# One level of block products in the last projection, its l by a product with ones, and a normalisation in one operation

## The chip, the cores and the metric

The kernel runs on one core of a Trainium2 chip. The metric is the device time of one execution in microseconds (us), the median of several; a profiled execution gives the span from first to last instruction, some 1.8 us less than its time. The mean granted TensorE clock was 0.996 to 1.000 of full speed in every run, and every run of a kernel with more than one was in the fast state. A kernel with a single run has no state of its own, which is said where it matters. The calls ran on different chips, and the median of the kernel before was 3249.5 to 3251.2 us in them; differences are taken within a call, and where kernels of different calls are compared, the text says so. Engines are written PE (matmul), PEld (its weight loads), DVE (VectorE), ACT (ScalarE), POOL (GpSimd) and SP (a DMA queue).

## The reference

```python
# x: (16, 512, 32, 32) float32
mu, var = mean and variance of x over each of 8 groups of 64 channels
xn = (x - mu) * rsqrt(var + 1e-5) * gamma + beta
q, k, v = split(qkv_w @ xn + qkv_b)               # 1x1 convolution, 3 x 512 channels
attn = softmax(q^T k * 128**-0.5)                 # 4 heads of 128, 1024 tokens
out = x + proj_w @ (attn-weighted v) + proj_b     # 1x1 convolution, residual
```

Everything is float32.

## The kernel before

The sixteen images follow each other in one stream: while the score products (`s`) and weighted sums (`po`) of one image run, the projection of the image before and the statistics, normalisation and v, q, k of the next are woven in between. `l` is the denominator of the softmax, a sum of exponentials for each token. Large products are made from block products: two levels for q, k and the projection (49 products of 256 columns in place of 64), one level for v (7 products of half size in place of 8). Block products need sums of blocks of the activations (`t1`, `t2`, ...) and of the results, which DVE makes. `warm` are matmuls without use that PE runs at the start while it waits.

The parts that the change touches:

```python
def apply(self, xn, x, mu, sc, c, on_scalar):          # first image: two passes
    nc.vector.tensor_scalar(xn, x, mu[c], sc[c], ALU.subtract, ALU.mult)
    if on_scalar:
        nc.scalar.activation(xn, xn, AF.Identity, bias=beta)
...
def normalise(b, c, half=None):                        # other images: two passes, both on ACT
    nc.scalar.activation(t, t, AF.Identity, bias=nmu[:, i])
    nc.scalar.activation(t, t, AF.Identity, bias=beta_sb[:, i], scale=sc[:, i])
...
def denominators(b, h):                                # l, every head of every image
    # DVE: transpose, reduce, three small additions, transpose
    nc.vector.reciprocal(r, l[:, 3, :])                # 32x32
    nc.sync.dma_start(row..., r)                       # to DRAM ...
    nc.sync.dma_start(rinv[b, h], row.to_broadcast((P, N)))   # ... and back as 128 equal rows
    nc.vector.scalar_tensor_tensor(worst, l[:, 3, :], 1.0, r, ALU.mult, ALU.max,
                                   accum_out=spans[:, i : i + 1])
...
# after the last score product: the last image's projection in two levels, nothing beside it
o_blocks(last)
run(groups[0])
divide(last, HEADS - 1)
sums_of_b(ob[last], (2,), (1,))
run(staggered(groups[1:]))
```

`spans` collects max(l, 1/l) of every head. If the total is over 1e20, a second, general path does the whole work again.

## Time and profile before

| what | before |
|---|---|
| time, median of 3 | 3251.3 us (3250.0 to 3251.66) |
| profiled span | 3247.3 us, clock 0.997 |
| PE busy | 3202.9 us, 99% |
| start, until the first v product | 17.71 us |
| one image | mostly 199.47 us |
| tail, from the end of the last score product | 49.67 us |

The span has three parts with different limits, so it is read in three parts. To mark the image borders I use the product `pm`, the first small matmul of an image's statistics, of which there is one an image: the second image has it at 143.42 us, the last at 2933.94. The totals of the page are these (busy us, share of the span, number of instructions):

```profile
PE 3202.9 (99%) x10708; PEld 2011.9 (62%) x10708; DVE 2476.6 (76%) x4425; ACT 1290.0 (40%) x2178; POOL 16.8 (1%) x20
```

They tell that PE is the bound almost everywhere, and nothing of where the one per cent that is not PE lies. That is at the two ends, and the prediction below starts from there.

### The profile page before, as it was taken

The numbers are of one execution on the slowest core, as the hardware profiler recorded it, in microseconds if no ns is written. First come the engines' busy times: TensorE is split into PE (matmuls) and PEld (weight loads), VectorE is DVE, ScalarE is ACT, GpSimd is POOL, SyncE is SP. The second block draws the span as 40 slices with busy tenths as digits, with TensorE's granted clock in tenths as the row PEclk, the third lists the DMA queues.
The fourth block names the chain that finished last, engine by engine and source line by source line (L and its number), as shares of the span: only waits on it lengthen the run. The fifth ranks groups of instructions, "written<-read, shape, count | busy, mean of one in ns | idle before, by whom it ended". The sixth has DMA issues, their size and how long they took to land.

```text
span 3247.3 us, 31121 instructions
## 1 busy us (share of the span) xinstructions
PE 3202.9 (99%) x10708; PEld 2011.9 (62%) x10708; DVE 2476.6 (76%) x4425; ACT 1290.0 (40%) x2178; POOL 16.8 (1%) x20
## 2 busy tenths in 40 slices
PE   7999999999999999999999999999999999999997
PEld 6566666666666666666666666666666666666654
DVE  8858688586886868868687785967859689586886
ACT  2433434334343343434434343443433434344332
POOL 0000000000000000000000000000000000000000
PEclk9999999999999999999999999999999999999998
DMA  5323333233232333333333332333323333233232
GB/s 174 128 79 126 111 104 131 77 118 123 95 129 87 117 111 107 119 103 112 107 114 109 102 123 90 120 108 113 123 80 126 105 111 124 84 114 123 80 115 83
DMA packets 114021, 357.39 MB, mean 110 GB/s; under 512 B 15424, under 2 KB 27200, under 8 KB 113856
## 3 DMA queue, kind: packets, MB, share of 16 engines
q1 hardware_dynamic: 112848, 354.27, 32.2%
q8 instruction: 86, 1.41, 0.2%
q10 hardware_dynamic: 1008, 1.06, 0.1%
q14 instruction: 79, 0.65, 0.1%
HBM read 310.00 MB, written 45.29 MB: 109 GB/s over the span
## 4 chain that ended last, share of the span: by engine, by line
PE 90%; ACT 5%; DVE 3%; DMA 1%; issue 1%; POOL 0%; ACTq 0%; SPq 0%; POOLq 0%; DVEq 0%
PE s L603 25%; PE po L648 25%; PE qk_x L466 12%; PE qk_y L466 9%; PE v_x L545 6%; PE v_y L545 5%; PE pp_x L466 5%; PE pp_y L466 3%; ACT x L232 2%; ACT x L231 2%; DVE tot L615 1%; ACT p L608 1%; DVE pp_r L498 1%; POOL rstd L64 0%; DVE pp_r L481 0%
## 5 line engine op out<-in xcount | busy, mean ns | idle before, releaser
L603 PE MATMUL s<-qk,qk 128*128 128x512 f32 x2048 | 1048.4, 593 | 2.2 <-DVE qk L516 1.3
L648 PE MATMUL po<-p,v 128*128 128x512 f32 x2048 | 1045.3, 593 | 0.7 <-ACT p L608 0.7
L608 ACT ACTIVATE p<-s 128x512 f32<-128x512 f32 x1024 | 611.2, 597 | 1053.2 <-PE s L603 1046.4
L615 DVE TENSOR_TENSOR tot<-tot,p 128x1024 f32<-128x1024 f32 x384 | 468.8, 1221 | 315.3 <-ACT p L608 312.1
L648 PEld LDWEIGHTS po<-p,v 128*128 128x128 f32 x2048 | 387.1, 190 | 455.0 <-issue 431.0
L603 PEld LDWEIGHTS s<-qk,qk 128*128 128x128 f32 x2048 | 386.2, 190 | 93.7 <-issue 37.3
L466 PEld LDWEIGHTS qk_x<-qk_t,w 128*128 128x128 f32 x1344 | 250.6, 190 | 199.4 <-issue 140.2
L466 PE MATMUL qk_x<-qk_t,w 128*128 128x256 f32 x1344 | 358.0, 383 | 1.4 <-ACT qk_u L394 1.1
L394 ACT COPY qk_u<-qk_x 128x512 f32<-128x512 f32 (+1 forms) x256 | 136.4, 533 | 240.6 <-PE qk_x L466 239.5
L466 PE MATMUL pp_x<-pp_t,w_proj 128*128 128x256 f32 x672 | 180.3, 385 | 1.1 <-ACT pp_u L394 1.1
L545 PE MATMUL v_y<-w_v,x 128*128 128x256 f32 x720 | 176.5, 381 | 3.8 <-ACT x L232 3.8
L545 PEld LDWEIGHTS v_y<-w_v,x 128*128 128x128 f32 x720 | 135.3, 190 | 66.3 <-issue 40.2
L481 DVE TENSOR_TENSOR qk_r<-qk_y,qk_u 128x512 f32<-128x512 f32 (+1 forms) x256 | 158.4, 619 | 22.8 <-PE qk_y L466 21.4
L466 PEld LDWEIGHTS pp_x<-pp_t,w_proj 128*128 128x128 f32 x672 | 125.1, 191 | 78.1 <-issue 51.7
L545 PEld LDWEIGHTS v_x<-w_v,xt 128*128 128x128 f32 x720 | 136.8, 190 | 57.0 <-issue 43.0
L545 PE MATMUL v_x<-w_v,xt 128*128 128x256 f32 x720 | 170.1, 379 | 0.0
L466 PE MATMUL qk_y<-x,w 128*128 128x256 f32 x512 | 141.8, 379 | 0.0
L516 DVE SCALAR_TENSOR_TENSOR qk<-qk_r,qkb_sb,qk_r 128x512 f32<-128x512 f32 x192 | 135.4, 745 | 1.5 <-ACT qk_r L479 0.4
L394 ACT COPY pp_u<-pp_x 128x512 f32<-128x512 f32 (+1 forms) x128 | 68.2, 533 | 170.0 <-PE pp_x L466 166.9
L565 DVE TENSOR_TENSOR v<-v_y,v_u 128x512 f32<-128x512 f32 x64 | 43.7, 682 | 114.4 <-ACT v_u L394 69.9
L481 DVE TENSOR_TENSOR qk_r<-qk_y,qk_p 128x512 f32<-128x512 f32 (+1 forms) x128 | 79.1, 618 | 57.1 <-PE qk_y L466 57.1
L466 PEld LDWEIGHTS qk_y<-x,w 128*128 128x128 f32 x512 | 97.3, 190 | 39.7 <-issue 21.8
(144 smaller groups left out, 3499.7 us busy)
## 6 DMA issues: line engine op xcount, KB each, us to landing
w<-kept SPq DMA_DIRECT2D x90, 896.0 KB, 4.5
w_v<-kept_v SPq DMA_DIRECT2D x60, 768.0 KB, 4.5
w_proj<-kept_proj SPq DMA_DIRECT2D x48, 896.0 KB, 4.6
rinv<-row SPq DMA_DIRECT2D x64, 512.0 KB, 3.7
y<-in_x SPq DMA_DIRECT2D x128, 256.0 KB, 3.8
out_y<-y SPq DMA_DIRECT2D x128, 256.0 KB, 2.4
x<-in_x SPq DMA_DIRECT2D x62, 512.0 KB, 4.1
w<-kept SPq DMA_DIRECT2D x30, 448.0 KB, 3.3
```

The lines of the kernel that those rows point to most:

```text
L231: nc.scalar.activation(t, t, AF.Identity, bias=nmu[:, i])
L232: nc.scalar.activation(t, t, AF.Identity, bias=beta_sb[:, i], scale=sc[:, i])
L394: nc.scalar.copy(t[n][:, :width], t["x"][:, :width])
L466: nc.tensor.matmul(acc[:, ts(i, Q)], have["w"][:, i, SLOTS[an], :], inner(i, bn), start=(first and i == 0), stop=True, skip_group_check=True,)
L481: nc.vector.tensor_add(dst, view(a), view(c))
L516: nc.vector.scalar_tensor_tensor(st[b, h][:, ts(half, HALF)], a[:, r, :], qkb_sb[:, i : i + 1], c[:, r, :], ALU.add, ALU.add,)
L545: nc.tensor.matmul(acc[:, ts(g, HC)], xb[b][bn][k][:, ts(2 * jj + g, P)], wi[:, k, :], start=(first and g == 0 and k == 0), stop=(k == KC ...
L565: nc.vector.tensor_add(dst, view(a), view(c))
L603: nc.tensor.matmul(sc, ks[b, h][:, ts(j, P)], qs[b, h][:, ts(half, HALF)], start=True, stop=True)
L608: nc.scalar.activation(ps[s][:, ts(half, HALF)], sc, AF.Exp, scale=SCALE)
L615: nc.vector.tensor_add(tot[b, h], tot[b, h], ps[s])
L648: nc.tensor.matmul(po[b, h][:, i], vs[b, h // 2][:, h % 2, j, :], ps[s][:, i], start=(j == 0), stop=(j == NB - 1),)
```

## The change

Its intent: the tail is bound by DVE and by two transfers, not by PE, so spend PE work to save the others there; the normalisation is one pass where it was two; and the first image's x is to land before the weights.

```diff
-        nc.vector.tensor_scalar(
-            xn, x, mu[:, c : c + 1], sc[:, c : c + 1], ALU.subtract, ALU.mult
-        )
+    def shift(self, mu, sc):                     # sh = beta - mu * sc, 128x4
+        nc.vector.tensor_mul(t, mu, sc)
+        nc.vector.tensor_sub(sh, self.beta, t)
...
+            self.nc.scalar.activation(xn, x, AF.Identity, bias=sh[:, i], scale=sc[:, i])
         else:
+            self.nc.vector.tensor_scalar(xn, x, sc[:, i], sh[:, i], ALU.mult, ALU.add)
... load_x
-            eng = (nc.sync, nc.scalar)[c % 2] if b == 0 else nc.sync
-            eng.dma_start(xs[b, c], x[b, ts(c, P), :])
+            for half in range(NH2 if b == 0 else 1):
+                i = ts(half, HALF) if b == 0 else ds(0, N)
+                nc.sync.dma_start(xs[b, c][:, i], x[b, ts(c, P), i])
... the last head's l
+        for half in range(NH2):
+            nc.tensor.matmul(l, ones_sq, t[:, ts(half, HALF)], start=True, stop=True)
+            nc.vector.reciprocal(r[:, i], l)
+            nc.vector.tensor_mul(os_[b, h][:, i], os_[b, h][:, i], r[:, i])
... and its check
+        nc.vector.reciprocal(l, r[:BLK, :])
+        nc.vector.scalar_tensor_tensor(l, l, 1.0, r[:BLK, :], ALU.mult, ALU.max, accum_out=...)
... the last projection: 28 products of 512 columns, residual and bias already in y
+            mm(x_[r], r, 1, True);  copy(r, "p1")
+        recip = last_division(b, HEADS - 1)
+        sums_of_b(bl, (2,), (1,))
+        ...  products 5, 2, 6 with their additions into y
+        last_span(recip)
+        ...  products 7, 4, 3
... start
-    warm(9, "warm")
+    warm(7, "warm")
```

The diff above leaves out three parts of the change: outside the first image too the halves are normalised with all four first halves ahead (before, tile by tile); in the first image DVE and ACT now take the tiles in turn, and only the first of the four weight sums of v is still placed by an order of its own (`issue_after`), where all four were; the last head's sum of exponentials is added in halves.

The last image's x is loaded into `y` early and the bias added there by ACT; outputs leave from `y` on two queues. The weights of the one-level products are stored once and loaded again for the last image.

More of the change, by code (lines that the diff above doesn't have):

```diff
@@ L49, in group @@
         nc.tensor.matmul(pm[:, :k], self.avg, mean, start=True, stop=True)
-        mu = gn.tile([P, k], F32, tag="mu", name="mu")
-        nc.vector.tensor_copy(mu, pm[:, :k])
         d = gn.tile([P, k], F32, tag="d", name="d")
-        nc.vector.tensor_sub(d, mean, mu)
+        nc.vector.tensor_sub(d, mean, pm[:, :k])
         d2 = gn.tile([P, k], F32, tag="d2", name="d2")
@@ L58, in group @@
         nc.vector.tensor_add(v, d2, mv[:, :, 1])
+        mu = gn.tile([P, k], F32, tag="mu", name="mu")
+        nc.vector.tensor_copy(mu, pm[:, :k])
         pv = self.ps.tile([P, HALF], F32, tag=self.tag, name="pv")
@@ L67, in group, with apply @@
         return mu, sc
-    def apply(self, xn, x, mu, sc, c, on_scalar):
-        nc, beta = self.nc, self.beta[:, c : c + 1]
-        nc.vector.tensor_scalar(
-            xn, x, mu[:, c : c + 1], sc[:, c : c + 1], ALU.subtract, ALU.mult
-        )
+    def shift(self, mu, sc):
+        nc = self.nc
+        t = self.gn.tile([P, self.ncc], F32, tag="t", name="t")
+        nc.vector.tensor_mul(t, mu, sc)
+        sh = self.gn.tile([P, self.ncc], F32, tag="sh", name="sh")
+        nc.vector.tensor_sub(sh, self.beta, t)
+        return sh
+    def apply(self, xn, x, sc, sh, c, on_scalar):
+        i = slice(c, c + 1)
         if on_scalar:
-            nc.scalar.activation(xn, xn, AF.Identity, bias=beta)
+            self.nc.scalar.activation(xn, x, AF.Identity, bias=sh[:, i], scale=sc[:, i])
         else:
-            nc.vector.tensor_scalar(xn, xn, beta, None, ALU.add)
+            self.nc.vector.tensor_scalar(xn, x, sc[:, i], sh[:, i], ALU.mult, ALU.add)
 @with_exitstack
@@ L183, in fast_path @@
     ones = one.tile([BLK, 1], F32, name="ones")
+    ones_sq = one.tile([P, P], F32, name="ones_sq")
     xs, xb, vs, qs, ks, os_, ob = {}, {}, {}, {}, {}, {}, {}
@@ L203, in fast_path @@
     nc.vector.memset(neghalf, -0.5)
+    nc.vector.memset(ones_sq, 1.0)
     for t, src in (
@@ L217, in stats_group, with normalise @@
         mu, sc = norm.group(mvs.pop(b))
-        nmu = None
-        if b > 0:
-            nmu = gn.tile([P, NCC], F32, tag="nmu", name=f"nmu_{b}")
-            nc.vector.tensor_scalar_mul(nmu, mu, -1.0)
-        scaled[b] = mu, sc, nmu
-    def normalise(b, c, half=None):
-        t = xs[b, c] if half is None else xs[b, c][:, ts(half, HALF)]
-        mu, sc, nmu = scaled[b]
-        if nmu is None:
-            norm.apply(t, t, mu, sc, c, True)
-        else:
-            i = slice(c, c + 1)
-            nc.scalar.activation(t, t, AF.Identity, bias=nmu[:, i])
-            nc.scalar.activation(t, t, AF.Identity, bias=beta_sb[:, i], scale=sc[:, i])
+        scaled[b] = sc, norm.shift(mu, sc)
+    def normalise(b, c, half):
+        t = xs[b, c][:, ts(half, HALF)]
+        sc, sh = scaled[b]
+        norm.apply(t, t, sc, sh, c, b > 0 or c % 2 == 1)
     def halves(tiles, prefix):
@@ L297, in fast_path @@
     store["v"] = kept.tile([P, 7, KC, HC], F32, name="kept_v")
+    store["last"] = kept.tile([P, 8, HALF], F32, name="kept_last")
     def stage_blocks(site):
@@ L342, in group_weights @@
                 nc.vector.tensor_sub(flat, st["a12"], st["s2"])
+            if site == "proj":
+                nc.sync.dma_start(store["last"][:, p], flat)
         def at(n):
@@ L373, in v_sums @@
     def v_sums():
-        nc.vector.tensor_add(wv["s1"], wv["a21"], wv["a22"])
         nc.vector.tensor_sub(wv["s2"], wv["s1"], wv["a11"])
@@ L594, in fast_path @@
     ps, tot, po, rinv, last_eviction = {}, {}, {}, {}, {}
+    steps = B * HEADS * NB
     def where(s):
@@ L608, in scores @@
         nc.scalar.activation(ps[s][:, ts(half, HALF)], sc, AF.Exp, scale=SCALE)
-        if half == 0 or j == 0:
+        i = ts(half, HALF) if s == steps - 1 else ds(0, N)
+        if j == 0 or (half == 0 and s < steps - 1):
             return
@@ L614, in scores @@
         else:
-            nc.vector.tensor_add(tot[b, h], tot[b, h], ps[s])
+            nc.vector.tensor_add(tot[b, h][:, i], tot[b, h][:, i], ps[s][:, i])
     def denominators(b, h):
@@ L641, in denominators, with last_division, last_span @@
         )
+    def last_division(b, h):
+        t = tot.pop((b, h))
+        for half in range(NH2):
+            l = ps_s.tile([P, HALF], F32, tag="s", name=f"l_{half}")
+            nc.tensor.matmul(l, ones_sq, t[:, ts(half, HALF)], start=True, stop=True)
+            i = ts(half, HALF)
+            r = lpool.tile([P, N], F32, tag="rinv", name=f"rinv_{b}_{h}") if half == 0 else r
+            nc.vector.reciprocal(r[:, i], l)
+            nc.vector.tensor_mul(os_[b, h][:, i], os_[b, h][:, i], r[:, i])
+        return r
+    def last_span(r):
+        l = lpool.tile([P, N // BLK, BLK], F32, tag="tt", name="l_last")
+        l = l.rearrange("p c m -> p (c m)")[:BLK, :]
+        nc.vector.reciprocal(l, r[:BLK, :])
+        nc.vector.scalar_tensor_tensor(
+            l, l, 1.0, r[:BLK, :], ALU.mult, ALU.max,
+            accum_out=spans[:, B * HEADS - 1 : B * HEADS],
+        )
     def weighted_sum(s, half):
@@ L652, in weighted_sum @@
         if j == NB - 1:
-            if half == 0:
+            if (b, h) not in os_:
                 os_[b, h] = opool.tile([P, N], F32, tag="o", name=f"o_{b}_{h}")
@@ L690, in staggered, with last_loads @@
         return [u for _, _, u in sorted(at, key=lambda t: t[:2])]
+    late = {}
+    def last_loads(what):
+        if what == "x":
+            late["y"] = []
+            for c in range(NCC):
+                t = xpool.tile([P, N], F32, tag="x", name=f"y_{c}")
+                nc.sync.dma_start(t, x[B - 1, ts(c, P), :])
+                late["y"].append(t)
+            return
+        late["w"] = []
+        for g in range(4):
+            t = qkpool.tile([P, N], F32, tag=f"qk{g % 2}", name=f"wl_{g}")
+            t = t.rearrange("p (i m) -> p i m", m=HALF)
+            first = 2 * g
+            n = slice(1, 2) if g == 0 else slice(0, 2)
+            nc.sync.dma_start(t[:, n], store["last"][:, first + n.start : first + 2])
+            late["w"] += [t[:, 0], t[:, 1]]
@@ new lines, in last_bias, with last_projection, mm, add @@
+    def last_bias():
+        for c in range(NCC):
+            nc.scalar.activation(
+                late["y"][c], late["y"][c], AF.Identity, bias=projb_sb[:, c : c + 1]
+            )
+    fine = []
+    def last_projection(b):
+        y, bl = late["y"], ob[b]
+        x_, y_, z_, kept_ = {}, {}, {}, {}
+        def mm(acc, r, p, first):
+            for k in range(KC):
+                nc.tensor.matmul(
+                    acc, late["w"][p][:, ds((r * KC + k) * P, P)], bl[FACTORS[p][1]][k],
+                    start=(first and k == 0), stop=(k == KC - 1), skip_group_check=True,
+                )
+        def add(row, r, half, a, done):
+            o = 2 * row + r
+            t = y[o][:, ts(half, HALF)]
+            nc.vector.tensor_add(t, t, a)
+            if done:
+                (nc.sync, nc.scalar)[r].dma_start(out[b, ts(o, P), ts(half, HALF)], t)
+        def copy(r, n):
+            t = upool.tile([P, HALF], F32, tag=n, bufs=1 if n == "u3" else 2, name=f"l_{n}_{r}")
+            nc.scalar.copy(t, x_[r])
+            kept_[n, r] = t
+        for r in range(2):
+            x_[r] = ps_a.tile([P, HALF], F32, tag="x", name=f"lx_{r}")
+            mm(x_[r], r, 1, True)
+            copy(r, "p1")
+        recip = last_division(b, HEADS - 1)
+        sums_of_b(bl, (2,), (1,))
+        for r in range(2):
+            y_[r] = ps_a.tile([P, HALF], F32, tag="y", name=f"ly_{r}")
+            mm(y_[r], r, 5, True)
+            add(0, r, 0, kept_["p1", r], False)
+        for r in range(2):
+            z_[r] = ps_s.tile([P, HALF], F32, tag="s", name=f"lz_{r}")
+            mm(z_[r], r, 2, True)
+            add(0, r, 0, z_[r], True)
+        for r in range(2):
+            mm(x_[r], r, 6, False)
+            copy(r, "u2")
+        last_span(recip)
+        for r in range(2):
+            add(0, r, 1, kept_["u2", r], False)
+        total = gn.tile([BLK, 1], F32, tag="total", name="total")
+        nc.vector.tensor_reduce(total, spans, AX.X, ALU.add)
+        for r in range(2):
+            mm(x_[r], r, 7, False)
+            copy(r, "u3")
+            add(1, r, 1, kept_["u3", r], False)
+            add(1, r, 1, y_[r], True)
+        most = ps_s.tile([P, HALF], F32, tag="s", name="most")
+        nc.tensor.matmul(most[:1, :1], total, ones, start=True, stop=True)
+        ok = gn.tile([1, 1], F32, tag="fine", name="fine")
+        nc.vector.tensor_scalar(ok, most[:1, :1], LIMIT, None, ALU.is_le)
+        fine.append(ok)
+        for r in range(2):
+            mm(x_[r], r, 4, False)
+            add(1, r, 0, x_[r], True)
+        for r in range(2):
+            mm(y_[r], r, 3, False)
+            add(0, r, 1, y_[r], True)
@@ L706, in plan_head @@
                 spread(plan, staggered(proj_groups(b - 1)), 0, NB)
-            if b + 1 < B:
+            if b + 1 == B:
+                plan[0].append(lambda: last_loads("x"))
+            else:
                 plan[0].append(lambda: load_x(b + 1))
@@ L710, in plan_head @@
                 plan[5].append(lambda: stats_group(b + 1))
-                plan[6] += [lambda c=c: normalise(b + 1, c) for c in range(NCC)]
+                plan[6] += [
+                    lambda c=c, half=half: normalise(b + 1, c, half)
+                    for half in range(NH2) for c in range(NCC)
+                ]
+        elif b + 1 == B:
+            if h == 2:
+                plan[0].append(lambda: last_loads("w"))
+                plan[2].append(last_bias)
+            else:
+                os_[b, h] = opool.tile([P, N], F32, tag="o", name=f"o_{b}_{h}")
+                plan[3].append(lambda: o_blocks(b))
+                plan[3].append(lambda: sums_of_b(ob[b], (1,)))
+                plan[4].append(lambda: sums_of_b(ob[b], (2,), (0,)))
         elif b + 1 < B:
@@ L741, in fast_path @@
     with tc.issue_after(before_power.ins):
-        v_sums()
+        nc.vector.tensor_add(wv["s1"], wv["a21"], wv["a22"])
+    v_sums()
     x_sums(0)
@@ L748, in fast_path @@
     stage_sums(1)
-    steps = B * HEADS * NB
     plan = []
@@ L758, in fast_path @@
             units = plan[j]
-        if s > 0 and s % NB == 0:
+        if 0 < s < steps and s % NB == 0:
             denominators(*where(s - 1)[:2])
@@ L771, in fast_path @@
             del ps[s - 1]
-    total = gn.tile([BLK, 1], F32, tag="total", name="total")
-    nc.vector.tensor_reduce(total, spans, AX.X, ALU.add)
-    most = ps_s.tile([P, HALF], F32, tag="s", name="most")
-    nc.tensor.matmul(most[:1, :1], total, ones, start=True, stop=True)
-    fine = gn.tile([1, 1], F32, tag="fine", name="fine")
-    nc.vector.tensor_scalar(fine, most[:1, :1], LIMIT, None, ALU.is_le)
-    nc.vector.tensor_scalar(flag, fine, -1.0, 1.0, ALU.mult, ALU.add)
-    last = B - 1
-    o_blocks(last)
-    groups = proj_groups(last)
-    sums_of_b(ob[last], (1,))
-    run(groups[0])
-    sums_of_b(ob[last], (2,), (0,))
-    divide(last, HEADS - 1)
-    sums_of_b(ob[last], (2,), (1,))
-    run(staggered(groups[1:]))
+    last_projection(B - 1)
+    nc.vector.tensor_scalar(flag, fine[0], -1.0, 1.0, ALU.mult, ALU.add)
 def general_path(ctx, tc, x, sources, out, consts, dims):
@@ L832, in general_path @@
         mu, sc = norm.group(mv)
+        sh = norm.shift(mu, sc)
         for c in range(NCC):
-            norm.apply(xn[c], xs[c], mu, sc, c, False)
+            norm.apply(xn[c], xs[c], sc, sh, c, False)
         for j in range(NB):
```

## The prediction

Of the reciprocal the profile of before has one form, on 32 columns (row `L632`, 335 ns); the durations of the tail's reciprocals are worked out from it.

> **What bounds the kernel now.** I read first the stretches of the span with each engine's busy time (columns: stretch, its length, then busy us and instructions of PE, weight loads, DVE, ACT and POOL, the granted PE clock, DMA share, GB/s), because a mean over the whole span hides its two ends.
>
> ```profile
> 0.00:20.00 20.00, 7.31 (x32) 6.76 (x33) 11.82 (x34) 4.54 (x7) 1.70 (x5) 1.00 0.84 277
> ...
> 600.00:800.00 200.00, 199.73 (x669) 125.53 (x668) 152.76 (x271) 81.14 (x137) 1.01 (x1) 1.00 0.32 109
> ...
> 3199.00:3247.30 48.30, 26.79 (x104) 19.14 (x102) 35.91 (x68) 9.60 (x18) 0.00 (x0) 0.82 0.39 129
> ```
>
> In the middle PE is busy 199.73 of 200 us: the sixteen images are bound by the matmuls, which the diff leaves alone until the last projection. What can be had lies in the first 20 us (12.7 us without a matmul) and in the last 48.3 us (21.5 us without one). Next the waits of PE (us in total, times, longest):
>
> ```profile
> PE pm L49 <- DVE mean L47: 11.8, 1, 11.8
> PE pp_y L466 <- DVE pp_r L481: 5.4, 2, 5.1
> PE pp_y L466 <- DVE o L658: 5.0, 1, 5.0
> PE v_y L545 <- ACT x L232: 3.8, 14, 0.3
> ```
>
> The first is the start (statistics of the first image), the next two are the tail, the fourth is all that the normalisation of the other images shows: 0.27 us each. Then the chain that ended last, in the tail:
>
> ```profile
> 3203.70 0.35 DVE r L632
> 3204.05 0.02 issue
> 3204.07 3.39 DMA row<-r
> 3207.46 0.02 issue
> 3207.48 4.21 DMA rinv<-row
> 3211.69 0.02 issue
> 3211.71 1.24 DVE o L658
> ...
> 3235.87 3.80 DMA y<-in_x
> ```
>
> The last head's reciprocal of l goes to DRAM and comes back as 128 equal rows, 7.6 us of transfers that nothing covers; later a reload of x, 3.8 us, stands in the chain [...]. In between DVE adds two levels of block products.
>
> [...] a pass with a bias took 1146 ns and one with scale and bias 1230 ns. [...] The trace has it on 32 columns only, where it is already slower than an addition of the same shape (335 against 176 ns). [...] granted clock 0.82 in the tail, and after the 5.0 us wait the first matmuls of 256 columns took 1.19 us for two instructions, 1.02 us being normal for two of 512. [...]
>
> ```profile
> L231 ACT ACTIVATE x<-x,nmu 128x1024 f32<-128x1024 f32 x60 | 67.1, 1146 | 0.0
> L232 ACT ACTIVATE x<-x,beta_sb,sc 128x1024 f32<-128x1024 f32 x60 | 69.7, 1230 | 16.4 <-DVE sc L66 16.4
> L588 DVE TENSOR_TENSOR y<-y,pp_r 128x512 f32<-128x512 f32 x128 | 83.7, 684 | 0.7
> L629 DVE TENSOR_TENSOR l<-l 32x32 f32<-32x32 f32 x64 | 11.3, 176 | 1.1
> L632 DVE RECIPROCAL r<-l 32x32 f32<-32x32 f32 x64 | 21.5, 335 | 1.2
> ```
>
> **The change, part by part.**
>
> Start. x comes before the weights, in 8 half tiles on one queue. Today the last statistics end at 11.6 us, because the second tile lands at 7.44. In the stretch from 4 to 8 us the DMA moved some 390 to 400 GB/s; x alone is 2 MB, about 5.3 us from 2.9 us on, so landed by 8.5 and its statistics done by 9.4: 2.2 us gained. One small DVE operation leaves the chain to pv (0.2), two enter behind sc (0.4), but the 0.7 us weight sum no longer stands ahead of x and there is one pass in place of two. With 7 warm matmuls instead of 9 (4.19 us for 9) the first product follows pv by 3.3 us instead of 3.85: 0.5 more. Given back: in the built order DVE makes four normalisations and four weight sums before the second t1, so the second matmul of product 5 must wait until about 5.3 us after the start, where PE gets to it at 3.9; with what follows I take off 1.7. Net 1.2 us.
>
> Images 1 to 15. ACT drops 60 passes of 1146 ns (4.6 us an image), but ACT is 40% busy and these ran before sc was there, so off the path. Behind sc the order now has an addition to tot (1.22), t, a 0.4 us block sum and sh: the first normalisation starts about 2 us later after sc, though one tot addition fewer stands ahead of ve, so sc comes 1.2 us sooner. Then 8 halves of about 0.6 take the same 4.6 us as 4 wholes, with all first halves first. The 0.27 us waits should go, but a matmul on t1 of the new order comes forward and may wait for DVE by about as much. I book 1 us for all 15, of 3.8 at most.
>
> Tail, from T = 0 at the end of the last score product (3197.63); the span ends 49.7 later. PE: 49 products of 256 columns become 28 of 512. At 0.86 us for 512 columns (score and weighted-sum products start 0.86 apart) that is 24.0 instead of 21.1 us, plus two products with ones, 1.7: 4.6 us more PE work. What goes are the 7.6 us of transfers, the reload and the two-level sums. By the built order: last weighted sums and product 1 until 6.0, l halves until 7.7, product 5 until 11.2. DVE is at the first reciprocal at 7.5. Its duration I must estimate: additions go from 176 ns at 32 columns to 684 at 512, 1.06 ns a column and 142 fixed; the reciprocal's 335 less 142 over 32 columns is 6 ns a column, so 3.2 us for 512 and 6.3 for 1024. So: two reciprocals until 13.9, two products with o until 15.2. Then, in the built order, the reciprocal of the check (32x1024) stands ahead of the second t2 sum: until 21.5, t2 at 22.2. PE finishes product 2 at 16.6 and idles to 22.25, 5.7 us, then runs cold, about 1.5 us lost. The remaining 14 products of 0.86 with that loss end at 35.7, the last addition at 36.6 (ACT's output transfer ahead of a copy costs perhaps 0.2). From the last addition to the end it is 4.7 us today (3242.6 to 3247.3), kept: 41.5. Gain 49.7 - 41.5 = 8.2 us.
>
> Sum: 1.2 + 1 + 8.2 = 10.4 us, so 3251.3 - 10.4 = about 3241.
>
> **The rivals.** First: the reciprocal takes a fixed extra and little per column (335 ns could be that). Then DVE is through at 12.5, PE has no gap, the tail ends at about 34: gain 15.5, time 3233. For it: only one width is in the trace. [...] Third: the new order of the middle puts a wait of 0.5 us or more into each of 15 images, 8 us lost, or takes away hidden ones (the v_x group took 2.31 us for eight instructions that need 1.72) and wins as much: 3249 or 3233. Fourth: the start is bound by all of its loads (5.5 MB in the first 20 us), so that x first only moves the wait to the weights: 1 to 2 us lost.
>
> **Range and chances.** The tail's gain lies between 3.7 and 15.5, the start between -1 and 3, the middle between -4 and 5. They hardly all go one way: 3231 to 3249 for 8 in 10. Two per cent is 65 us, more than the whole tail; only a stall repeated in each image, over 4 us, could reach it. Faster 0.01, same 0.98, slower 0.01.
>
> **What would show it.** In the changed profile: RECIPROCAL of 128x512 at 3.2 us and of 32x1024 at 6.3; a PE wait of 5 to 6 us for ot ahead of product 6's second half, with cold matmuls behind; no transfer row or rinv for the last head; first v_x product at about 14.3 instead of 17.7; a middle stretch still near 199.7 of 200. I am wrong if the reciprocals differ by half, if PE shows new waits in every image, or if the DMA of the first 15 us holds the weights back.

## The result and the profile after

The changed kernel took 3237.09 us, the median of 4 runs (3236.77 to 3238.22), against 3251.21 of the kernel before in the same rounds (3250.0 to 3251.66). Ratios here are the mean time of one kernel's fast runs over that of the other's of the same rounds, so not quite the ratio of the medians: 0.9958, with a 95% interval of 0.9941 to 0.9975. By the measure of 2% that is the same time, 14 us quicker. The profiled spans went from 3247.3 to 3235.1 us, 12.2; the profiled execution of before was itself some 2 us quicker than its median.

The page's totals after:

```profile
PE 3203.1 (99%) x10666; PEld 2005.6 (62%) x10666; DVE 2466.3 (76%) x4392; ACT 1246.7 (39%) x2168; POOL 16.3 (1%) x20
```

PE's busy time did not move (3202.9 to 3203.1), so the whole gain is idle time of PE that went away. ACT's 43 us less were no gain by themselves. The stretches, with the columns that the prediction explains:

```profile
0.00:20.00 20.00, 7.43 (x34) 6.95 (x35) 12.49 (x36) 5.00 (x7) 1.22 (x5) 1.00 0.76 237
...
600.00:800.00 200.00, 199.84 (x671) 126.17 (x670) 153.54 (x273) 78.04 (x136) 1.01 (x1) 1.00 0.32 111
...
3199.00:3235.10 36.10, 25.22 (x55) 9.93 (x53) 25.95 (x26) 2.93 (x5) 0.00 (x0) 0.91 0.17 61
```

The first 20 us have hardly more PE work in them than before (7.43 against 7.31), though two `warm` matmuls, 0.9 us, have gone from them. The middle rose from 199.73 to 199.84 of 200 us. The last stretch begins at the same time in both profiles, not at the same work; counted from the last score product the tail went from 49.67 us at a mean clock of 0.83 to 41.99 at 0.92. PE's waits after (us in total, times, longest):

```profile
PE pm L49 <- DVE mean L47: 11.9, 1, 11.9
PE lx L756 <- DVE ot L253: 5.3, 1, 5.3
PE pp_y L469 <- DVE pp_r L484: 2.3, 14, 0.2
```

The wait of the start is as long as it was. The tail's long waits for DVE (5.1 and 5.0) became one of 5.3. The 14 waits of the v products for ACT's normalisation are gone, and 14 others, smaller, have come. The chain that ended last, in the tail (start, us, what):

```profile
3200.71 6.48 DVE rinv L656 x2
3207.19 1.14 DVE o L657 x2
3208.33 6.45 DVE l_last L664
3214.78 0.56 DVE ot L253
...
3215.38 7.11 PE lx L756 x12
...
3222.60 3.63 PE lx L756 x8
3226.24 3.45 PE ly L756 x8
...
3229.71 0.69 DVE y L764
```

No transfer is left in it up to the last addition, which ends at 3230.40; the 4.7 us from there to the end, with the last outputs in them, are as long as before. In place of the transfers stand three reciprocals, `rinv` twice and `l_last`, 12.9 us of the 42. The rows of the reciprocals (busy us, then mean ns of one):

```profile
L656 DVE RECIPROCAL rinv<-l 128x512 f32<-128x512 f32 x2 | 6.6, 3323 | 0.0
L664 DVE RECIPROCAL l_last<-rinv 32x1024 f32<-32x1024 f32 x1 | 6.5, 6533 | 0.0
```

Split by the marks, the 12.2 us of the two profiled spans lie here (the end of the last score product is read as the start of the matmul behind it):

| part | before | after | gained |
|---|---|---|---|
| start of the span to `pm` of the second image | 143.42 | 142.84 | 0.58 |
| from there to `pm` of the last image | 2790.52 | 2786.52 | 4.00 |
| from there to the end of the last score product | 263.69 | 263.75 | -0.06 |
| tail | 49.67 | 41.99 | 7.68 |

### The profile page after: what moved, and what is told of

Same layout as the page of the kernel before. It is cut to its first block, busy times and chain, and to the rows that moved or that the text cites. A ratio compares the mean times of both kernels' runs of the same rounds, so it can differ in the third digit from the quotient of the medians.

```text
span 3235.1 us, 31036 instructions
## 1 busy us (share of the span) xinstructions
PE 3203.1 (99%) x10666; PEld 2005.6 (62%) x10666; DVE 2466.3 (76%) x4392; ACT 1246.7 (39%) x2168; POOL 16.3 (1%) x20
## 4 chain that ended last, share of the span: by engine, by line
PE 92%; DVE 6%; ACT 1%; POOL 0%; issue 0%; DMA 0%; SPq 0%; DVEq 0%; POOLq 0%
PE s L607 25%; PE po L675 25%; PE qk_x L469 12%; PE qk_y L469 9%; PE v_x L548 7%; PE v_y L548 5%; PE pp_x L469 5%; PE pp_y L469 4%; DVE tot L620 2%; DVE y L588 1%; DVE y L591 1%; DVE pp_r L501 1%; POOL rstd L64 0%; PE lx L756 0%; DVE pp_r L484 0%
## 5 line engine op out<-in xcount | busy, mean ns | idle before, releaser
L469 PE MATMUL pp_x<-pp_t,w_proj 128*128 128x256 f32 x630 | 167.8, 383 | 0.0
L469 PEld LDWEIGHTS pp_x<-pp_t,w_proj 128*128 128x128 f32 x630 | 117.2, 190 | 73.7 <-issue 44.5
L469 PEld LDWEIGHTS qk_y<-x,w 128*128 128x128 f32 x512 | 97.3, 190 | 39.7 <-issue 21.5
```

Source lines behind the costliest of these rows:

```text
L469: nc.tensor.matmul(acc[:, ts(i, Q)], have["w"][:, i, SLOTS[an], :], inner(i, bn), start=(first and i == 0), stop=True, skip_group_check=True,)
```

## The experiments

My theory after this result: the tail is worth what the two transfers and the reload had cost, less the check's reciprocal, which stands alone on the chain; the normalisation is worth some 4 us by the waits that it takes from PE in each image; the start is worth next to nothing, because eight issues on a single queue hold x back. Rivals: the reciprocal lies beside PE work that would be needed anyway and costs nothing; the 4 us of the middle are chance, or come from the tail's new weights; the start's halves are slow because of their size (2 KB rows), not because of the queue.

### The tail alone

The kernel before with the new last projection only; normalisation and start as they were.

> The kernel before with the new last projection alone (start and normalisation as before). If the three parts of the change add up, the tail alone gives what the traces put in it: from the last score product to the end 42.0 us instead of 49.7, so a span near 3239.6 against 3247.3, a time 7 to 8 us below the kernel before, an image still 199.47 us long and the first v_x product still at 17.7 us. Rival: the tail owes part of its gain to the other two parts (loads and buffers that come free earlier); then the tail stays above 44 us here.

Measured: 3244.21 us (16 runs, 3243.62 to 3246.3), before 3250.74 (29 runs), ratio 0.9981 (0.9974 to 0.9988): 6.5 us, a little under the 7 to 8 expected. The tail took 42.8 us, with the same wait of 5.3 us of `lx` for `ot`. The images stayed at 199.4 to 199.5 us (2791.60 us between the marks), with the 0.27 us waits for ACT as before. So the tail by itself is worth 6.5 us, and the new weights bring the middle nothing: it is 1.1 us longer here, of which a wait that is named below makes 0.9.

### The normalisation alone

The kernel before with the one-pass normalisation only.

> The kernel before with the one-pass normalisation alone (order of the loads and tail as before). Mine: the middle of the changed kernel gained 4.0 us because the one pass with halves in front takes the wait for x out of each image: here an image is again near 199.22 us instead of 199.47, the wait of v_y for ACT x is gone, and the time is 4 to 5 us below the kernel before. Rival: the middle gained by the other parts or by chance of placement; then an image stays at 199.4 or more and the time within 1.5 us of before.

Measured: 3247.6 us (12 runs, 3246.76 to 3249.07), before 3250.74 in the same rounds, ratio 0.999 (0.9982 to 0.9999): 3.1 us, under the 4 to 5 expected, and only just clear of nothing. In the profile an image is again mostly 199.22 us, as in the changed kernel and as expected. Between the marks 2787.84 us, 2.7 less than in the profile of before, and the waits for ACT's `x` are gone. That the middle's gain comes from the normalisation is shown by the length of an image: 199.22 us in every kernel here with the new one, 199.47 in both without. The old tail took 51.7 us in this profile: `row` and `rinv` took 3.99 and 4.37 us, 3.39 and 4.21 in the profile of before. In these two profiles the old tail's length moves with its transfers; the new one has none on its chain before the last addition.

### l for the check copied, no second reciprocal

The check needs l itself. The changed kernel makes it as 1/(1/l) with a third reciprocal. Here ACT copies 32 rows of l out of PSUM instead.

```diff
         for half in range(NH2):
             nc.tensor.matmul(l, ones_sq, t[:, ts(half, HALF)], start=True, stop=True)
+            nc.scalar.copy(kl[:, i], l[:BLK, :])
             nc.vector.reciprocal(r[:, i], l)
...
-        nc.vector.reciprocal(l, r[:BLK, :])
```

> The changed kernel, but the check of l takes l as ACT copies it out of PSUM (two copies of 32x512) instead of as a second reciprocal of 32x1024 on DVE; same check, result unchanged. Mine: that reciprocal, 6.53 us in the order of DVE ahead of the second t2 sum, makes the PE wait of 5.3 us and the cold matmuls behind it: without it the wait falls below 1 us, the granted clock in the tail rises, the tail goes from 42.0 to about 35 us, the time is 6 to 7.5 us below the changed kernel. Rival: the two reciprocals of 3.3 us and the products behind them bound the tail anyway, and the gain is under 3 us.

Measured: 3230.58 us (5 runs, 3230.38 to 3232.53), ratio to before 0.9937 (0.9924 to 0.9951), correct. The chain in its tail:

```profile
3203.01 6.58 DVE rinv L659 x2
3209.59 0.04 issue
3209.64 2.84 PE lz L756 x6
3212.48 0.04 issue
3212.51 5.50 PE lx L756 x12
```

The two reciprocals stay, `l_last` is gone from DVE, and PE goes from `lz` to `lx` without a wait: the twelve instructions of `lx` took 5.50 us where they had taken 7.11 behind the wait. The tail is 35.55 us, 6.4 less than 41.99. So the rival that the reciprocal of the check lies beside needed work is wrong: 6.5 us of DVE cost 6.4 us of the tail, and the time fell by as much. This version beats both kernels: its ten runs, in two calls, lie between 3230.38 and 3232.53 us, the nine of the changed kernel, in two other calls, between 3236.77 and 3239.28.

### The check's reciprocal later

If the reciprocal only stands in the wrong place, ordering it behind the last `t2` sum should free most of that. Moving the call in the source left the built order as it was, so it is tied behind the sum.

```diff
         sums_of_b(bl, (2,), (1,))
+        after_sums = last_sub[0]
...
-        last_span(recip)
+        with tc.issue_after(after_sums.ins):
+            last_span(recip)
```

> The changed kernel with the check's reciprocal kept but ordered behind the second t sums on DVE. If its place were all that counts, the tail would be as short as in the run without it (about 35 us). I expect half of it: PE goes on to product 6 without a wait of 5 us, but then the additions that stand behind the reciprocal and the product of the check, which waits for it, stop PE for 3 to 4 us before the last products: tail about 38.5 us.

Measured: 3236.44 us, a single run, span 3234.7; the tail 41.7 us, so the expected gain did not come. PE's waits in this kernel:

```profile
PE most L806 <- DVE total L799: 3.6, 1, 3.6
...
PE lx L758 <- ACT l_u L772: 1.1, 1, 1.1
```

The wait for `ot` is gone, and its time came back. The chain shows what ran on DVE after the reciprocal, an addition to `y` that began as it ended:

```profile
3211.64 6.45 DVE l_last L666
3218.09 0.55 DVE y L766
```

From 3211.64 to 3218.09 no addition to `y` ran, so the three copies `l_u` that ACT had begun from 3210.87 to 3213.53 were not read. ACT's next copy, whose buffer (`bufs=1`) is read by an addition that ended at 3221.11, began at 3221.20, and `lx` on PE waited 1.1 us for it; `most`, the sum of the check, waited 3.6 us for DVE's `total`. In both places that were tried the 6.5 us of DVE are on the tail's path; of the three versions only the one that takes them off DVE gains more than 0.3 us. A third place, behind still more of the additions, was not tried.

### The start: whole tiles, and two queues

In the changed kernel the statistics of the first image end no earlier (the copy `mean` starts at 11.70 us, 11.62 before), though the weights are asked for from 6.68 us on only, and from 1.67 us before. Over all profiles here with the changed start it begins between 11.24 and 11.78 us, with the old start between 11.26 and 11.62. Two variants of its start: x in four whole tiles on the one queue, and x in halves on two queues.

```diff
 # whole tiles
-            for half in range(NH2 if b == 0 else 1):
-                ...
+            nc.sync.dma_start(xs[b, c], x[b, ts(c, P), :])
 # two queues
-                nc.sync.dma_start(xs[b, c][:, i], x[b, ts(c, P), i])
+                eng = (nc.sync, nc.scalar)[half] if b == 0 else nc.sync
+                eng.dma_start(xs[b, c][:, i], x[b, ts(c, P), i])
```

> The changed kernel with x of the first image as four whole tiles (packets of 4 KB a row) on the one queue, instead of eight halves (2 KB). The changed kernel moved some 290 GB/s from 4 to 8 us where the kernel before moved 390 to 403, and its statistics ended at 11.7 us instead of the 9.4 that I had forecast. If the halves' smaller packets slow the transfers, the rate here is again above 360 GB/s and the statistics end before 10.5. Rival: the one queue with its waits between issues, or the small constants beside it, hold x back; then the rate stays near 300 and the statistics end at 11.3 or later.

> The changed kernel with first halves of x on one queue and second halves on the other, x still ahead of the weights, and the small constants behind x on the second queue. If packets of 2 KB are the limit, the rate stays near 300 GB/s and the statistics end at 11 us or later; if the single queue and its waits (5.9 us for eight issues) or the constants are, x has landed by 9 us and the statistics end before 10.5. The built order moves the weight sums ahead of the normalisation, so the first product is not compared.

Measured, one run each beside 3251.23 of before: whole tiles 3237.11 us, two queues 3236.16. What the DMA moved between 4 and 8 us (last column, GB/s), first in the changed kernel:

```profile
4.00:6.00 2.00, 0.00 (x0) 0.00 (x0) 1.69 (x4) 0.00 (x0) 0.00 (x0) 1.00 0.90 286
6.00:8.00 2.00, 0.00 (x0) 0.00 (x0) 1.66 (x4) 0.00 (x0) 0.00 (x0) 1.00 0.95 298
```

and with the same halves on two queues:

```profile
4.00:6.00 2.00, 0.00 (x0) 0.00 (x0) 1.57 (x3) 0.14 (x1) 0.00 (x0) 1.00 1.00 371
6.00:8.00 2.00, 0.00 (x0) 0.00 (x0) 1.49 (x4) 0.00 (x0) 0.00 (x0) 1.00 1.05 400
```

Halves on two queues moved 371 and 400 GB/s, so the size of the rows is not the limit; whole tiles on the one queue moved 399 and 360, so one queue by itself is not either. What is left, by elimination, is the eight issues on one queue. They stand in the timeline of the changed kernel:

```profile
0.76 5.88 SPq L199 DMA_DIRECT2D x<-in_x  x8
```

and of the variant with two queues:

```profile
0.75 1.86 ACTq L200 DMA_DIRECT2D x<-in_x  x4
0.76 1.81 SPq L200 DMA_DIRECT2D x<-in_x  x4
```

The one queue needed 5.88 us for its eight issues, with waits in between (1.6 us for `gamma` and 1.0 us for earlier pieces of x); four issues on each of two queues needed 1.9, four whole tiles on one 4.17. What makes an issue of x wait for `gamma` the trace does not tell. In both variants the statistics ended at 10.55 and 10.59 us, 1.1 us earlier than 11.70. The first v product followed at 15.59 and 16.59 us, after 16.73. With two queues it waited 0.76 us for x, because in that built order DVE had all four weight sums ahead of its passes on x (the first began at 13.30 us, the passes at 16.00). With whole tiles its eight instructions took 2.72 us where the changed kernel's took 1.91, but a second profile of the changed kernel, below, shows 2.45 for the same eight, so that is not the whole tiles' doing. At `pm` of the second image the two variants stood at 142.36 and 141.63 us; the changed kernel at 142.84, and at 143.54 in its second profile. A one-run difference of 1 us in time settles nothing, so two queues and DVE's order were timed on the best kernel; whole tiles were not.

### The start on the best kernel

The kernel with l copied, run again as the comparison; the same with two queues; and that with the weight sums ordered behind DVE's four passes on x:

```diff
-    with tc.issue_after(before_power.ins):
+    with tc.issue_after(norm.last_dve.ins):
         nc.vector.tensor_add(wv["s1"], wv["a21"], wv["a22"])
-    v_sums()
+        v_sums()
```

> The same kernel as e3, as the comparison for the two beside it: within 1 us of e3's 3230.6 us, first product of the second image's statistics at about 143.3 us.

> e3 with x in halves on two queues. If the 1.1 to 1.7 us that the two-queue start had gained when the second image's statistics begin lasts to the end: 3229.0 to 3229.5 us, with that product at 141.6 to 142.2. If later waits eat it: 3230.6, no difference from e3. The last matmul stretch as in e3 (35.5 us from the end of the last score product).

> As e7, with the four weight sums of v ordered behind DVE's four passes on x. If DVE's place in line is what holds the first v product in e7 (there 16.6 us, with a wait of 0.76 us for x): the first v product at 15.6 us and another 0.5 us gained, 3228.5 to 3229. If only the second pass of work (t1, t2 sums behind the same DVE) counts: first product at 15.6, but the waits move to the products on t1, and the time stays within 0.3 us of e7.

Measured, five runs each, before at 3250.89 us (9 runs):

| kernel | time, range | first v product | `pm` of the second image |
|---|---|---|---|
| l copied, again | 3231.16 (3230.38 to 3231.66) | 16.82 | 142.90 |
| two queues | 3231.39 (3229.32 to 3231.67) | 16.71 | 143.65 |
| two queues, sums behind | 3229.91 (3229.49 to 3230.6) | 15.85 | 141.94 |

Two queues alone gained nothing in time, against the first of my two expectations: the statistics ended at 10.21 us, 1.6 earlier, but DVE stood 0.98 us at the first weight sum for a weight that had not landed, and the first v product came when it had come before. Its eight instructions then took 3.78 us. The same start had been faster on the changed kernel (first line: two queues on the changed kernel; second: on the best one):

```profile
16.59 1.99 PE L549 MATMUL v_x<-wv_a,x 128*128 128x256 f32 x8 [0.76 <-DVE x L84]
16.71 3.78 PE L549 MATMUL v_x<-wv_a,x 128*128 128x256 f32 x8 [1.27 <-DVE x L84]
```

These 1.8 us are nearly all of the 2.0 by which the two profiles differ at `pm` of the second image (141.63 and 143.65). What makes the same eight products slow in one execution and not in another stays open; the mean granted clock over the whole execution is 0.999 in the one and 1.000 in the other.

With the weight sums behind x the first product is 1 us earlier and the time 1.25 us less than the comparison, with ranges that overlap by 0.2 us, and 0.7 less than the same comparison kernel in its first call; I had expected 3228.5 to 3229. That DVE's order decides what the earlier landing is worth is therefore not shown: with that order unchanged, two queues on the changed kernel came to `pm` of the second image at 141.63 us, as early as the 141.94 with the sums behind. The last kernel has the lowest median of the study, 21 us under the one before (ratio 0.9935, 0.9921 to 0.9948).

### The new start against the old one

The tail alone and the normalisation alone gained 6.5 and 3.1 us, together 9.6 of about 14. This run tells whether the rest lies in the start: the changed kernel with the old start, beside the changed kernel again.

> The changed kernel itself, as the comparison for the one beside it: 3236.8 to 3238.2 us as before.

> The changed kernel with the old start alone put back (x in whole tiles on two queues, nine warm matmuls, the weight sum in its old place), so new normalisation and new tail together. The tail alone had gained 6.5 us, the normalisation alone 3.1, the whole change about 14. Theory A, read from the traces: the start is worth only 0.6 us and the parts of the middle and the tail are worth more together than each by itself: 3237.5 to 3238.2 us. Theory B: the parts add up, and the missing 4 us lie in the start: about 3241 us.

Measured: changed kernel again 3237.75 us (3236.91 to 3239.28), with the old start 3238.21 (3236.47 to 3239.19), before 3249.51 (9 runs). Both have the ratio 0.9964 (0.9951 to 0.9978). The difference of the medians, 0.5 us, is far inside the spread of either. So the new start is worth nothing that five runs can show, and theory B, which put 4 us there, falls: every one of the five runs lies under its 3241. Tail and normalisation together gained 11.3 us in this call, 1.7 more than the two by themselves in theirs. The noise allows such a gap: by the intervals of the ratios the tail gained 3.9 to 8.5 us, the normalisation 0.3 to 5.9, both 7.1 to 15.9. If it is real, part of it can be a wait that stands once, of a score product for ACT's `p`: 1.8 us in both partial kernels, 0.9 in the kernel before, 0.5 in this one. That it adds up to the gap is argued from the profiles and not shown; what sets this wait stays open.

## Why the prediction was right, and where it was not

The time of 3241 us was 4 too high, inside the range of 3231 to 3249, and the verdict of no change over 2% held. By its steps:

**Start, 1.2 us predicted, 0.6 by the marks, none by the timed comparison.** The step that failed is "x alone is 2 MB, about 5.3 us from 2.9 us on, so landed by 8.5 and its statistics done by 9.4". It took the rate of the old start's four whole tiles on two queues, 390 to 400 GB/s, for eight halves on one queue, which moved 286 to 298; the eight issues alone took 5.88 us. The statistics ended at 11.70. The first v product came at 16.73, not 14.3 (the prediction's own terms, 2.2, 0.2 and 0.5 off 17.7, give 14.8, and its net of 1.2 rests on these); what it gained on 17.71 lies after the statistics. In both profiles PE goes from the `warm` matmuls to the first v product without a wait, and two of them fewer (3.30 us for 4.19) are 0.9 of the 1.0 us gained. That x was ready for it (POOL's `rstd` took 1.01 us where it had taken 1.50, the weight sum no longer stood ahead of x, and x needs one pass) is what let the cover be shorter. Afterwards the second matmul on `t1` waited as predicted, though 0.46 us and not 1.4, and 0.58 was left at the second image, less than the 0.7 by which the changed kernel's two profiles differ there.

**Images 1 to 15, 1 us predicted "of 3.8 at most", 4.0 measured.** The mechanism was right and the size was not. The waits for ACT went, and new ones came, as the prediction said. But the new ones (2.3 us, the 14 waits of `pp_y`) are smaller than those removed, and more was hidden than I had allowed. In the products on the second image, before:

```profile
353.46 2.31 PE L545 MATMUL v_x<-w_v,x 128*128 128x256 f32 x8
...
356.47 0.70 PE L545 MATMUL v_y<-w_v,x 128*128 128x256 f32 x2 [0.27 <-ACT x L232]
```

and after:

```profile
350.57 5.75 ACT L82 ACTIVATE x<-x,sh,sc 128x512 f32<-128x512 f32 x8 [1.95 <-DVE sh L75]
...
352.77 1.89 PE L548 MATMUL v_x<-w_v,x 128*128 128x256 f32 x8
```

The eight `v_x` instructions took 2.31 us with x coming one tile at a time, and take 1.89 now that all first halves come first. This stretching was in the prediction only as a rival ("takes away hidden ones ... and wins as much"); it belonged in the sum. In most images it is smaller than in this one. From `pm` of the fourth image to `pm` of the fifth, the starts of the v products lie 0.50 us closer in all (0.27 of it the listed wait), the matmuls ahead of the new wait 0.23 further apart, and the image is 0.26 shorter (199.48 to 199.22). Fourteen times 0.25 are 3.5 of the 4.0 us. One step was off and did not matter: I had taken 0.6 us for a half pass of ACT; eight took 5.75 us, 0.72 each.

**Tail, 8.2 us predicted, 7.7 between the two profiles.** Here the working held step by step, though "transfers that nothing covers" was too strong: PE stood for 5.0 of their 7.6 us. That DVE would run in the order of the built program was my assumption; `rinv`, `o`, `l_last` and `ot` did (from 3200.62, 3207.10, 3208.25 and 3214.71 us). Counted from the end of the last score product (3193.11): first reciprocal at 7.6 (7.5 predicted), both done at 14.1 (13.9), the products with o done at 15.2 (15.2), the check's reciprocal done at 21.7 (21.5), matmuls again at 22.3 (22.25). The reciprocals took 3323 and 6533 ns (3.2 and 6.3 us predicted), so the slope read from one row of 32 columns (335 ns) and the fixed part of an addition was right: 3210 ns more for 512 columns more are 6.3 ns a column, on 128 partitions in the one and 32 in the other. PE's wait was 5.3 us (5.7). The mis-sized term is the loss after the wait, which I had estimated at 1.5 us without working it out (in the profile of before, behind the wait of 5.04 us that ended at 3213.08, the granted clock was 0.50 from 3214 to 3216): twelve instructions took 7.11 us where 0.43 each would be 5.16, so 1.95 and not 1.5, with small rests behind it. The granted clock was 0.50 for the first 3 us of them, and without the wait, in the run with l copied, the same twelve took 5.50, so 1.6 of the 1.95 went with the wait. The last addition ended at 37.3 and not 36.6; the issue of ACT's first output, put at 0.2 us, took 0.36. From there to the end it took 4.7 us, as before. The wait of 5.3 us and the loss of 1.6 make 6.9; the copy of l made the tail 6.4 shorter.

**The rivals.** A reciprocal with only a fixed extra would have shown some 0.84 us on 512 columns (an addition's 684 ns and the 159 that the small one took more); the rows say 3.3. The 3.7 us at the low end of the tail's range was an estimate of mine that no run here shows. A wait of 0.5 us in every image did not come: the new ones are 0.16. The other half of that rival, hidden waits that go, came in part (above). The fourth rival, a start bound by all of its loads, is not what happened: no v product of the start waits for a weight in the changed profile, and two queues moved more than the changed kernel in the same 4 us (371 and 400 GB/s against 286 and 298).

**The sum.** Predicted 10.4; the two profiles differ by 12.2, the medians by 14.1 in the first rounds and by 11.8 in the last. The term that made most of the difference is the middle, +3.0; start and tail together were 1.1 too high.

## What to carry to other kernels

Look for long instructions on the engine that a tail waits for, and ask for each whether its result can be had another way: here an inverse of an inverse cost 6.4 us, which a copy on ACT (busy 6.43 of the 35.55 us of that tail) removed; moving it to one other place in the order removed 0.3. A gain at the start of a chain (x landing earlier) has to be followed to a mark behind it, and in more than one execution: the same start, profiled in two kernels that differ in their tails alone, differed there by 2.0 us, more than the gain looked for. When a wait inside a steady loop is removed, count the stretching of the instructions beside it too, not only the wait that is listed.
